# A two-layer graph kernel: where the block turns of the first hidden state stand in layer 1's first step

## The chip, the cores and the metric

The kernel runs on one core of one Trainium2 chip. The metric is the device time of one execution in microseconds. Five engines work side by side, each on its own queue: TensorE (PE, matmuls, with the weight loads listed apart as PEld), VectorE (DVE), ScalarE (ACT), GpSimd (POOL) and SyncE (SP), which here issues nearly all DMA transfers.

## What is computed

Sixteen batches of a 1024 x 128 matrix `x` go through two layers, all in float32. `adj` is a symmetric-pattern 1024 x 1024 matrix. Layer 0 is one graph convolution with a residual and a layer norm. Layer 1 is a gated graph unit that runs five steps, again with a residual and a layer norm:

```python
x = _layernorm(x + (adj @ (x @ w0) + b0))

def step(h, _):
    m_in = m_out = adj @ h            # in_matrix = out_matrix = adj
    av = jnp.concatenate([m_in, m_out], axis=-1)
    u3 = h @ u3_w.T + u3_b
    z = jax.nn.sigmoid(av @ w3_w.T + w3_b + u3)
    r = jax.nn.sigmoid(av @ w4_w.T + w4_b + u3)
    hv = jnp.tanh(av @ w5_w.T + w5_b + (r * h @ u5_w.T + u5_b))
    return (1.0 - z) * h + z * hv, None

h = x                                  # five steps
x = _layernorm(x + h)
```

The heavy part is the product `adj @ h`, once in layer 0 and five times in layer 1, for each of sixteen batches.

## The kernel before

**Tiling and stages.** The sixteen batches are worked on in four groups ("quads") of four. Layer 0 runs over the quads `q` = 0 to 3 first, and layer 1 then runs over the quads, five steps each. One step is an aggregation (`aggregate`, the product with `adj`) followed by the gates. The layer 0 projection of a quad is done inside the aggregation after it, through hooks: functions that are called at given places in the list of products. So layer 0's projection of the last quad falls into the aggregation of layer 1's first step (tag `0_0`), and it is in this stage that the change lies.

**The aggregation.** The product with `adj` is computed by a Strassen-Winograd scheme on two levels. The outer level has seven products, which run as four *chains*: (1, 2), (3,), (6, 7) and (5, 4). Each chain computes one or two outer products by seven inner products, in the order 1, 5, 6, 2, 7, 3, 4. The right-hand operands of the outer products 4 to 7 are sums that VectorE writes into `tsum`; the right-hand operands of the inner products 4 to 7 are four sums each, written by `inner_sums` (L328 to L331) into `inner0` for the chains (1, 2) and (6, 7), and into `inner1` for (3,) and (5, 4). Inner products are collected in three PSUM banks `pa`, `pc` and `pb`. When a product is finished it is evicted by a copy on ScalarE or by an addition on VectorE: L407 after product 1, L408 after 5, L409 after 6, L410 after 2 and L413 after 4 on ScalarE; L411 after 7 and L412 after 3 on VectorE. Product 3 reuses the bank of product 5, so it cannot start before L408 has emptied it.

**Where the results go.** The results of chain (6, 7) are written into `rows[:, 0:2]`, those of chain (5, 4) into `rows[:, 2:4]`. `rows` has until then held the quad's input, and in layer 1's first step this input is the first hidden state h, with nodes as rows. The gates need h in another layout, in `hid`. In every later step the gates themselves produce that layout; only the first h has to be brought there. This is what `to_hidden(k)` does for batch k of the quad: `turn_hidden` makes four block transposes ("turns", L643, each of 128 x 256) of `rows[:, k]` into two stage buffers in the upper halves of `agg`, sends each buffer to DRAM with one DMA (L647), and `fetch_hidden` reads it back into `hid[:, k]` with four DMAs (L655). The stage buffers are `agg[:, 2 * (k % 2) + f, HALF:]`, so batch 2 reuses those of batch 0 and batch 3 those of batch 1. Eight turns read `rows[:, 0]` and `rows[:, 1]`, eight read the other two. Until the turns of the rows 0 and 1 have run, chain (6, 7) may not write its first result there, which is L408.

**What sets the order.** A scheduler orders each engine's instructions; the place of a statement in the program is what it goes by first, and it may move an instruction forward where it expects a wait. Instructions that went through `keep_in_program_order` keep the program's order among themselves on their engine. In this stage the program has, in this order: the sums of chain (6, 7), chain (3,) with its hooks, the sums of chain (5, 4), chain (6, 7) with its hooks, chain (5, 4).

**The other work of the stage.** VectorE also does the statistics of layer 0's last layer norms (L267, L269). ScalarE applies them (L286, 128 x 128 each), in `ypad` for two batches and in place in `hid` for the other two, and SP stores those results to `saved` (L292) before `hid` is overwritten by the fetches of batches 2 and 3. The gates of the same step start right behind chain (5, 4) and read `hid` first in L535.

Of the kernel before, what the change touches and what calls it, by code (L numbers as in the profile page):

```python
# [20 lines left out]
def kernel(  # L21
# [32 lines left out]
    nc = tc.nc  # L54
# [3 lines left out]
    HALF = N // 2  # L58
# [13 lines left out]
    rows = const.tile([P, QUAD, N], F32, name="rows")  # L72
    hid = const.tile([P, QUAD, N], F32, name="hid")
    agg = const.tile([P, QUAD, N], F32, name="agg")
# [36 lines left out]
    def load(q, dst, src_of, ks=range(QUAD)):  # L111
        for k in ks:
            nc.sync.dma_start(dst[:, k], src_of(q * QUAD + k))
# [13 lines left out]
    for i, c in enumerate([0, 1, "x0", "x1", *range(2, C), "x2", "x3"]):  # L127
        queue = queues[i % 2 if i < 6 else 0]
        if isinstance(c, str):
            k = int(c[1])  # L130
# [222 lines left out]
    def outer_sums(src, early=True, late=True, pinned=False):  # L353

        lo, hi = src[:, 0:2], src[:, 2:4]
        put = tc.keep_in_program_order if pinned else lambda op: op
        if early in (True, "hi"):
            op = put(nc.vector.tensor_sub(tsum[:, 2], hi[:, :, HALF:], hi[:, :, :HALF]))
        if early in (True, "lo"):
            op = put(nc.vector.tensor_add(tsum[:, 1], tsum[:, 2], lo[:, :, :HALF]))  # L360
        if late:
            put(nc.vector.tensor_sub(tsum[:, 0], hi[:, :, :HALF], lo[:, :, :HALF]))
            op = put(nc.vector.tensor_sub(tsum[:, 3], lo[:, :, HALF:], tsum[:, 1]))
        return op

    def behind_closing():

        return tc.issue_after(closed[0].ins) if closed[0] else nullcontext()
# [173 lines left out]
    def gate_seed(u):  # L542
        pin(nc.scalar.copy(seeded[u % 2], pus[u]))
# [5 lines left out]
    def gate_r(u, rest=True):  # L549

        k, h = UNITS[u]
        rh, cols, pu = rh_of[k % 2], ts(h, HALF), pus.pop(u)
        in_order(nc.tensor.matmul(  # L553
            pu, w_t["w4"], agg[:, k, cols], start=False, stop=True, skip_group_check=True
        ))
        pin(nc.scalar.activation(rh[:, cols], pu, AF.Sigmoid, bias=br))  # L556
        if rest:
            gate_rh(u)

    def gate_rh(u):  # L560
        k, h = UNITS[u]
        rh, cols = rh_of[k % 2], ts(h, HALF)
        pin(nc.vector.tensor_mul(rh[:, cols], rh[:, cols], hid[:, k, cols]))  # L563

    def gate_z(u):
        k, h = UNITS[u]
        cols, pz = ts(h, HALF), seeded[u % 2]
        in_order(nc.tensor.matmul(  # L568
            pz, w_t["w3"], agg[:, k, cols], start=False, stop=True, skip_group_check=True
        ))  # L570
        pin(nc.scalar.activation(z_of[k % 2][:, cols], pz, AF.Sigmoid, bias=bz))  # L571
# [39 lines left out]
    def turn_rows(k, h=None, to=None):  # L611
        cols, n = half_of(h)
        to = between(k, h) if to is None else to
        t = ypad[k % 2][:, cols]
        op = nc.vector.transpose(
            t.rearrange("p (to n j c) -> p n to c j", to=4, n=n, c=2),
            hid[:, k, cols].rearrange("p (n to i c) -> p n to c i", to=4, n=n, c=2),
        )
        tc.keep_in_program_order(nc.sync.dma_start(
            to.rearrange("g p x -> p g x"), t.rearrange("p (g x) -> p g x", x=64)  # L620
        ))
        return op
# [8 lines left out]
                dst[ts(to, SQ), cols].rearrange("j (m x) -> j m x", x=64), src[to]  # L631
            ))

    def turn_hidden(k, y, stage):

        v = y.rearrange("p (n c a j) -> p a n c j", n=4, c=2, a=4)
        w = 4 // len(stage)
        for f, t in enumerate(stage):
            if w == 4:
                nc.vector.transpose(t.rearrange("p (a n i c) -> p a n c i", a=4, n=4, c=2), v)  # L640
            else:
                for a in range(w):
                    nc.vector.transpose(  # L643
                        t[:, ts(a, QT)].rearrange("p (n i c) -> p n c i", n=4, c=2),
                        v[:, w * f + a],
                    )
            nc.sync.dma_start(  # L647
                hidden[k][ts(f, 4 * w)].rearrange("g p x -> p g x"),
                t.rearrange("p (g x) -> p g x", x=64),
            )  # L650

    def fetch_hidden(k):
        src = hidden[k].rearrange("(a n) (b j) x -> a j (n b) x", a=4, b=4)
        for a in range(4):
            nc.sync.dma_start(  # L655
                hid[ts(a, SQ), k].rearrange("j (m x) -> j m x", x=64), src[a]
            )

    def to_hidden(k):
        turn_hidden(k, rows[:, k], [agg[:, 2 * (k % 2) + f, HALF:] for f in range(2)])  # L660
        fetch_hidden(k)

    def turn(name, k, h):
# [27 lines left out]
    def call(f, *args):  # L691
        return lambda: f(*args)


    def projections(q):

        room = rooms[q % 2]
        ys = [ypad[0], ypad[1], room[:, 2], room[:, 3]]
        for k in (2, 3):
            nc.sync.dma_start(ys[k], x_rows(q * QUAD + k))  # L700
        hooks = {a: [call(project, q, k, ys[k])] for k, a in enumerate((5, 2, 3, "end"))}
        hooks.update({a: [seed_bias] for a in (1, 6, 7, 4)})
        return hooks
# [246 lines left out]
    for q in range(NQ):  # L950
        for s in range(STEPS):
            tag = f"{q}_{s}"
            if s == 0:
                if q == 0:
                    hooks = {
                        12: projections(NQ - 1),
                        3: {5: [call(to_hidden, 0)], 2: [call(to_hidden, 1)]},
                        67: {
                            3: [call(drain, 99, 0), call(to_hidden, 2)],
                            "end": [call(to_hidden, 3)],  # L960
                        },
                        54: {},
                    }
                    hooks[12][6] += [call(sums_of, rows, (3,)), call(outer_sums, rows, False, True)]
                else:
                    outer_sums(rows)
                    hooks = {54: {}}
            else:
                hooks = {54: {}}
            last = s == STEPS - 1  # L970
            end = last and q == NQ - 1

            k = s if q else s - 1
            if q < NQ - 1 and 0 <= k < QUAD:
                hooks[3] = {1: [call(next_load, q + 1, k)]}
                hooks[67] = {1: [call(next_turn, k)]}
            if q > 0 and s > 0:
                hooks.setdefault(67, {})[5] = [call(close_load, q - 1, s - 1)]
                hooks[54] = {6: [call(close, q - 1, s - 1)]}
            if q == s == 0:  # L980
                hooks[54][3, (0,)] = [call(gates_begin, tag, 3)]
            hooks[54][4] = [call(gate_r, 0, False)]
            hooks[54][3, (1,)] = [call(gate_z, 0)]
            aggregate(tag, rows, hooks, s > 0)
            if end:
                load(q, rows, saved_rows)
            elif last:
                load(q + 1, rows, saved_rows)
            with behind_closing():
                gate_rh(0)  # L990
            if not end:
                gate_seed(2)
            gate_r(1)
            gate_z(1)
            if end:
                turns[0] = part_of[2]
                ending(q, tag)
                break

            def updated(k):  # L1000
                if last:
                    turn_rows(k, None, closing[k])
                    fetch_hidden(k)
                elif k < 3:
                    turn_rows(k)
                    if k < 2:
                        fetch_rows(k)

            def step_update(u, part):
                k, h = UNITS[u]  # L1010
                if last and u == 4:
                    sums_of(rows, (1, 2))
                    sums_of(rows, (3,))
                update_half(tag, k, h, part, not last and k == 3)
                if u % 2:
                    updated(k)

            for u in range(3, 8):
                gate_first(tag, u, (u - 3) % 3)
                step_update(u - 3, (u - 2) % 3)  # L1020
                gate_r(u - 1)
                gate_z(u - 1)
            step_update(5, 2)
            gate_r(7)
            gate_z(7)
            step_update(6, 0)
            step_update(7, 1)
            part_of.insert(0, part_of.pop())
            then = f"{q}_{s + 1}" if not last else f"{q + 1}_0"
            gates_begin(then, 2 if q == NQ - 1 and s == STEPS - 2 else 3)  # L1030
            if not last:
                fetch_rows(3, 1)
                fetch_rows(3, 0)
# [32 lines left out]
```

## Time and profile before

| | us |
|---|---|
| median of three runs | 1766.96 |
| lowest and highest run | 1766.76, 1766.97 |
| the profiled execution, whole | 1767.13 |
| its span, first to last instruction | 1764.9 |
| TensorE busy in the span | 1753.4 |
| VectorE busy | 1302.2 |
| ScalarE busy | 800.8 |

The span is what the trace shows; the whole time is a little longer. Times in the traces are microseconds from the span's start. The chains (6, 7) and (5, 4) of layer 1's first step lie at about 234 to 263 us.

A timeline line reads: start, duration, engine, source line, operation, output<-input, shape, count, and in brackets the idle time before it with what ended it. A line of the waits reads: who waited, for whom, then total us, times, longest. In the chain of waits a line is start, duration and what ran; "issue" stands for time in which nothing that the profile shows was waited for.

### The profile page before, as it was taken

How to read it: one execution, taken by the hardware profiler on the slowest of the kernel's cores; microseconds unless marked ns; L12 is line 12 of the kernel's file. 1: busy time of each engine (PE TensorE's matmuls, PEld its weight loads, DVE VectorE, ACT ScalarE, POOL GpSimd, SP SyncE). 2: the span in 40 equal slices, each digit the busy share in tenths (PEclk: the TensorE clock that was granted, in tenths of full speed). 3: DMA queues.
4: the chain of work that ended last, by engine and by line, in shares of the span. 5: the costliest groups of instructions: out<-in, count | busy, mean ns of one | idle time of the engine just before them, and what ended most of it. 6: DMA issues, size and time to landing. Idle time of an engine off the chain costs nothing.

```text
span 1764.9 us, 19957 instructions
## 1 busy us (share of the span) xinstructions
PE 1753.4 (99%) x6709; PEld 1264.9 (72%) x6709; DVE 1302.2 (74%) x2286; ACT 800.8 (45%) x1425; POOL 110.4 (6%) x153
## 2 busy tenths in 40 slices
PE   9999999999999999999999999999999999999998
PEld 8888885776858577685867758576675857668584
DVE  7977777676776857777778667777778577777778
ACT  4355554344353433435354452535445353443537
POOL 2312320000000000000000000000000000000004
PEclk9999999999999999999999999999999999999999
DMA  9244354051332505143351424324243240514232
GB/s 266 75 139 144 120 142 109 12 119 34 86 69 67 140 18 136 39 118 75 81 132 60 108 60 96 87 69 119 58 110 101 55 94 26 131 25 107 60 84 95
DMA packets 405604, 161.86 MB, mean 92 GB/s; under 512 B 388352, under 2 KB 389504, under 8 KB 405504
## 3 DMA queue, kind: packets, MB, share of 16 engines
q1 hardware_dynamic: 402960, 153.01, 34.2%
q0 software_dynamic: 1968, 5.77, 1.3%
q10 hardware_dynamic: 576, 1.84, 0.3%
q8 instruction: 53, 0.87, 0.2%
q14 instruction: 47, 0.39, 0.1%
HBM read 94.51 MB, written 65.01 MB: 90 GB/s over the span
## 4 chain that ended last, share of the span: by engine, by line
PE 99%; DMA 1%; DVE 0%; POOL 0%; issue 0%; SPq 0%; POOLq 0%; ACT 0%; DVEq 0%
PE pb L425 25%; PE pc L425 14%; PE pa L425 14%; PE pu L553 8%; PE ph L576 8%; PE ph L577 8%; PE pu L535 8%; PE seeded L568 8%; PE pc_x L425 3%; PE pa_x L425 3%; PE seeded L509 2%; DMA agg<-in_adj_dram 1%; PE pt_adj L200 0%; PE pt L667 0%; PE pt_end L941 0%
## 5 line engine op out<-in xcount | busy, mean ns | idle before, releaser
L425 PE MATMUL pb<-e,inner 128*128 128x256 f32 x864 | 206.2, 379 | 0.0
L592 DVE TENSOR_TENSOR tsum<-tsum,hid 128x512 f32<-128x512 f32 x158 | 108.7, 688 | 106.1 <-ACT tsum L587 106.0
L587 ACT ACTIVATE tsum<-ph,bh 128x512 f32<-128x512 f32 x158 | 108.5, 687 | 164.6 <-PE ph L577 164.5
L425 PEld LDWEIGHTS pb<-e,inner 128*128 128x128 f32 x864 | 167.7, 194 | 19.0 <-ACT first L409 0.3
L553 PE MATMUL pu<-agg,w_t 128*128 128x512 f32 x320 | 163.7, 593 | 0.0
L576 PE MATMUL ph<-agg,w_t 128*128 128x512 f32 x320 | 163.4, 592 | 0.0
L568 PE MATMUL seeded<-agg,w_t 128*128 128x512 f32 x320 | 163.4, 592 | 0.0
L577 PE MATMUL ph<-tsum,u_t 128*128 128x512 f32 x320 | 163.4, 592 | 0.0
L535 PE MATMUL pu<-hid,u_t 128*128 128x512 f32 x320 | 157.0, 592 | 0.0
L556 ACT ACTIVATE tsum<-pu,br 128x512 f32<-128x512 f32 x160 | 110.0, 687 | 85.6 <-PE pu L553 85.6
L425 PE MATMUL pb<-s,inner 128*128 128x256 f32 x576 | 148.0, 379 | 0.0
L425 PE MATMUL pb<-a,inner 128*128 128x256 f32 x576 | 144.0, 379 | 0.0
L563 DVE TENSOR_TENSOR tsum<-tsum,hid 128x512 f32<-128x512 f32 x160 | 110.3, 689 | 38.1 <-ACT tsum L556 38.1
L425 PE MATMUL pc<-e,inner 128*128 128x256 f32 x560 | 133.9, 379 | 0.0
L425 PEld LDWEIGHTS pb<-s,inner 128*128 128x128 f32 x576 | 110.7, 194 | 23.7 <-issue 10.9
L571 ACT ACTIVATE tsum<-seeded,bz 128x512 f32<-128x512 f32 x160 | 110.0, 687 | 29.4 <-PE seeded L568 29.4
L425 PEld LDWEIGHTS pb<-a,inner 128*128 128x128 f32 x576 | 111.8, 194 | 12.7 <-DVE first L411 0.4
L425 PEld LDWEIGHTS pc<-e,inner 128*128 128x128 f32 x560 | 109.2, 195 | 12.8 <-PE pu L535 0.7
L577 PEld LDWEIGHTS ph<-tsum,u_t 128*128 128x128 f32 x320 | 60.8, 190 | 76.5 <-issue 59.1
L576 PEld LDWEIGHTS ph<-agg,w_t 128*128 128x128 f32 x320 | 60.6, 190 | 75.1 <-issue 74.4
L535 PEld LDWEIGHTS pu<-hid,u_t 128*128 128x128 f32 x320 | 60.8, 190 | 73.5 <-issue 72.2
L593 DVE TENSOR_TENSOR tsum<-tsum 128x512 f32<-128x512 f32 x158 | 109.2, 691 | 4.9
(201 smaller groups left out, 2860.9 us busy)
## 6 DMA issues: line engine op xcount, KB each, us to landing
turned<-ypad SPq DMA_DIRECT2D x48, 512.0 KB, 3.8
rows<-turned SPq DMA_DIRECT2D x192, 128.0 KB, 2.9
hvs<-saved SPq DMA_DIRECT2D x24, 512.0 KB, 4.1
rows<-saved SPq DMA_DIRECT2D x20, 512.0 KB, 3.8
hid<-hidden SPq DMA_DIRECT2D x64, 128.0 KB, 3.4
turned<-ypad SPq DMA_DIRECT2D x32, 256.0 KB, 2.9
rows<-turned SPq DMA_DIRECT2D x128, 64.0 KB, 2.1
hidden<-ypad SPq DMA_DIRECT2D x12, 512.0 KB, 4.0
```

The costliest lines, as they stand in the source:

```text
L425: product = nc.tensor.matmul(bank_of[a][:, ts(o, QT)], chunk(a, o, c), left[n][a][:, c, :], start=(a in (1, 5) and o == 0 and c == 0), sto ...
L535: in_order(nc.tensor.matmul(pu, w_t["u3"], hid[:, k, ts(h, HALF)], start=True, stop=True, skip_group_check=True))
L553: in_order(nc.tensor.matmul(pu, w_t["w4"], agg[:, k, cols], start=False, stop=True, skip_group_check=True))
L556: pin(nc.scalar.activation(rh[:, cols], pu, AF.Sigmoid, bias=br))
L563: pin(nc.vector.tensor_mul(rh[:, cols], rh[:, cols], hid[:, k, cols]))
L568: in_order(nc.tensor.matmul(pz, w_t["w3"], agg[:, k, cols], start=False, stop=True, skip_group_check=True))
L571: pin(nc.scalar.activation(z_of[k % 2][:, cols], pz, AF.Sigmoid, bias=bz))
L576: in_order(nc.tensor.matmul(ph, w_t["w5"], agg[:, k, cols], start=True, stop=False))
L577: in_order(nc.tensor.matmul(ph, w_t["u5"], rh_of[k % 2][:, cols], start=False, stop=True))
L587: pin(nc.scalar.activation(hv, ph, AF.Tanh, bias=bh))
L592: pinned(nc.vector.tensor_sub(hv, hv, hid[:, k, cols]))
L593: pinned(nc.vector.tensor_mul(hv, hv, z_of[k % 2][:, cols]))
```

## The change

Three things are moved, and nothing is added to or taken from the work:

- The turns of batch 0, called by a hook of chain (3,) before its product 5, are called before product 1 of chain (6, 7). Those of batch 1, called before product 2 of chain (3,), are called before product 5 of chain (6, 7). Both then stand behind the sums of chain (5, 4) in the program.
- The turns of batch 2 keep their hook, before product 3 of chain (6, 7) and so behind the eviction of product 7, but now go through `keep_in_program_order`, so that they hold this place against other instructions that do the same.
- Batch 3 is unchanged.

```diff
-    def turn_hidden(k, y, stage):
+    def turn_hidden(k, y, stage, pinned=False):
...
                 for a in range(w):
-                    nc.vector.transpose(
+                    op = nc.vector.transpose(
                         t[:, ts(a, QT)].rearrange("p (n i c) -> p n c i", n=4, c=2),
                         v[:, w * f + a],
                     )
+                    if pinned:
+                        tc.keep_in_program_order(op)
...
-    def to_hidden(k):
-        turn_hidden(k, rows[:, k], [agg[:, 2 * (k % 2) + f, HALF:] for f in range(2)])
+    def to_hidden(k, pinned=False):
+        stage = [agg[:, 2 * (k % 2) + f, HALF:] for f in range(2)]
+        turn_hidden(k, rows[:, k], stage, pinned)
         fetch_hidden(k)
...
                         12: projections(NQ - 1),
-                        3: {5: [call(to_hidden, 0)], 2: [call(to_hidden, 1)]},
                         67: {
-                            3: [call(drain, 99, 0), call(to_hidden, 2)],
+                            1: [call(to_hidden, 0)],
+                            5: [call(to_hidden, 1)],
+                            3: [call(drain, 99, 0), call(to_hidden, 2, True)],
                             "end": [call(to_hidden, 3)],
                         },
```

In the built program this gives three differences. On VectorE the eight turns of batches 0 and 1, which stood together ahead of the sums of chain (5, 4), now stand behind L328, L330 and L329 of that chain: one of them, then L331, then the other seven. The turns of batch 2, which were spread around L331 and L411, now follow L411. On TensorE the first two matmuls of product 1 of chain (5, 4), which stood ahead of product 4 of chain (6, 7), now stand behind it. On ScalarE L413 of chain (6, 7) moves ahead by one L286. The order of the transfers on SP and of POOL's instructions is the same.

## The prediction

> **What bounds the kernel now.** I read the page first, then the chain of waits around the stage that the diff touches, then the timelines of VectorE, ScalarE and TensorE there. The page:
>
> ```profile
> PE 1753.4 (99%) x6709; PEld 1264.9 (72%) x6709; DVE 1302.2 (74%) x2286; ACT 800.8 (45%) x1425; POOL 110.4 (6%) x153
> ...
> PE 99%; DMA 1%; DVE 0%; POOL 0%; issue 0%; SPq 0%; POOLq 0%; ACT 0%; DVEq 0%
> ```
>
> TensorE is busy for 99% of the span and the chain that ended last is TensorE nearly throughout. So a microsecond in which TensorE stands still is a microsecond of the result, and work on another engine costs nothing until TensorE waits for it. The list of all waits has only four lines for TensorE in the whole run; three belong to the first 12 us. The fourth is the place of this change. The waits and the chain, both for 236 to 258 us:
>
> ```profile
> ACT rows L408 <- issue: 3.4, 1, 3.4
> ...
> PE pc L425 <- ACT rows L408: 0.3, 1, 0.3
> ```
>
> ```profile
> 239.13 1.37 issue
> 240.50 0.59 ACT rows L408
> 241.10 0.04 issue
> 241.14 1.13 PE pc L425 x4
> ```
>
> The reader is to see that ScalarE's L408 (it empties bank c after product 5 of chain 67) sat idle for 3.4 us for a reason which the profile does not name ("issue"), and that TensorE's product 3, which reuses bank c, then waited for L408. The timeline of VectorE shows what L408 was held by:
>
> ```profile
> 237.09 0.69 DVE L331 TENSOR_TENSOR inner<-tsum,inner 128x512 f32<-128x512 f32 x1
> 237.71 2.72 DVE L643 STREAM_TRANSPOSE agg<-rows 128x256 f32<-128x256 f32 x8
> 240.35 0.65 DVE L328 TENSOR_TENSOR inner<-tsum 128x512 f32<-128x512 f32 x1
> 240.92 0.68 DVE L330 TENSOR_TENSOR inner<-tsum 128x512 f32<-128x512 f32 x1
> 241.52 0.68 DVE L329 TENSOR_TENSOR inner<-tsum,inner 128x512 f32<-128x512 f32 x1
> 242.12 0.43 DVE L643 STREAM_TRANSPOSE agg<-rows 128x256 f32<-128x256 f32 x1
> 242.49 0.65 DVE L331 TENSOR_TENSOR inner<-tsum,inner 128x512 f32<-128x512 f32 x1
> 243.06 0.76 DVE L643 STREAM_TRANSPOSE agg<-rows 128x256 f32<-128x256 f32 x2
> 244.11 0.69 DVE L411 TENSOR_TENSOR rows<-pb,rows 128x512 f32<-128x512 f32 x1 [0.29 <-PE pb L425]
> ```
>
> The eight turns of batches 0 and 1 read `rows[:, 0]` and `rows[:, 1]`; L408 writes into those same two rows. The eighth turn ends at 237.71 + 2.72 = 240.43, L408 starts at 240.50. In the listing of the program's order L408 waits for a count of VectorE that the eighth turn supplies. TensorE's side:
>
> ```profile
> 238.95 1.03 PE L425 MATMUL pa<-s,tsum 128*128 128x256 f32 x4
> 239.82 1.03 PE L425 MATMUL pa<-a,tsum 128*128 128x256 f32 x4
> 241.14 1.13 PE L425 MATMUL pc<-e,tsum 128*128 128x256 f32 x4 [0.30 <-ACT rows L408]
> ```
>
> Four matmul records take 239.82 - 238.95 = 0.87 us from start to start, so product 3 could have begun at 240.69; it began at 241.14. The whole loss in this stage today is 0.45 us. That is also all that any reordering here can win on this wait.
>
> [...]L408's stall stopped ScalarE altogether from 237.1 to 240.5 us, with the evictions L409 and L410 behind it. [...]The trace before shows clock 1.00 even in the window 8 to 12 us, where TensorE was busy for only 2.79 of 4 us; a longer gap isn't shown. [...]here the issues of `hidden<-agg` land after a median of 3.7 us, and I use that.
>
> **The change part by part.** No instruction is added or removed; work only moves.
>
> *VectorE.* In the changed program's order the three sums L328, L330, L329 of chain 54 stand ahead of the first turn, then one turn, then L331, then the other seven turns of batches 0 and 1. L331 waits for the last product of chain 3, which ran near 233 us, so this wait is empty. From 237.71 the new sequence, with start-to-start times from the rows above: L328 0.57 (240.35 to 240.92), L330 0.60, L329 0.60, which puts the first turn at 239.48; turn 0.37 (242.12 to 242.49), L331 0.57 (242.49 to 243.06), so that the seven others begin at 240.42. A turn's pitch is (240.35 - 237.71)/8 = 0.33; seven take 2.31, and the last one ends 0.08 beyond its pitch, as now. The eighth turn ends at 240.42 + 2.31 + 0.08 = 242.81 in place of 240.43: 2.38 later.
>
> *ScalarE and TensorE.* L408 still waits for the eighth turn of rows 0 and 1: in the changed program its VectorE count is again supplied by just that turn. So L408 starts at 240.50 + 2.38 = 242.88 and product 3 at 241.14 + 2.38 = 243.52. TensorE has nothing else to do: its order before product 3 is the same in both programs[...]. The gap grows from 0.45 to 2.83 us. **This term, +2.38 us, is the forecast's core.** The sums that move forward win nothing: their first reader, product 5 of chain 54, runs at 248.15, over 5 us behind them.
>
> *Product 4 of chain 67.* In the changed order the two matmuls of the next chain's product 1 no longer stand between products 3 and 4. Product 4 needs bank b emptied by L411. Now product 7 issues until 243.84, L411 starts 0.27 later and takes 0.69, ending at 244.80; product 3's second half covers only up to 244.70, and the two matmuls covered the rest. Without them TensorE waits 244.80 + 0.05 - 244.70, about 0.15. Bounds: 0 to 0.3 us.
>
> *The cover behind it.* ScalarE runs back to back from 240.50 to 253.41 (three evictions, 24 L286 of about 0.40 each with L413 and L407 among them, then L408 and L409), and TensorE's product 7 of chain 54 already waits for that L409: records of 0.87 from 252.47 would reach it at 253.34, it begins at 253.46. The 0.15 above therefore goes partly into a wait that exists anyhow. Added up on ScalarE: four of the five L286 ahead of L413 are left, ready at 249.04; product 4 ends at 243.52 + 4 x 0.865 + 0.15 + 1.73 = 248.86, L413 at 249.12 (+0.08); three L286 and L407 end near 251.38; nine L286 and L408 bring L409 to 255.32, 0.11 over a pure shift of 252.83 + 2.38. So TensorE leaves the stage 2.38 + 0.1 = about 2.5 us late. Between 2.3 (no extra wait) and 2.8 (both extra waits in full).
>
> *The third batch's turn, pinned.* Its first turn waits for the landing of a store of batch 0 and now stands behind P7's eviction L411 rather than ahead of it. Before, it did not hold anything: L411 waited 0.29 us for TensorE and VectorE was otherwise busy. Gain 0. It now stands ahead of L412: the store, issued 2.38 later than at 238.49, lands near 240.87 + 3.7 = 244.6, while L411 starts at about 246.4. Cost 0; bounds 0 to 0.3.
>
> *SP's queue.* Its order is unchanged. The first store of a turned block is issued when its two turns are done, 240.83 in place of 238.45, so all eight stores and sixteen fetches slip by the same 2.4. Batch 1 of `hid` lands now near 248.5 + 3.1 = 251.6 and is first read at about 257.0; TensorE slips as far, so the margin of 5 us stays. The stores of batches 2 and 3 follow SP's `saved<-hid` copies, which follow ScalarE's L286, also 2.4 to 2.5 later. L489, at 262.13, needs the first of these landed (252.86 + 3.7 = 256.6): 5 us spare, both moving. POOL's queue isn't passed: its last L283 of the stage is done at 239.3.
>
> *The sum.* 1767.13 us (the profiled execution's own time; its span is 1764.9 and 2.2 lie around it) + 2.5 = 1769.6. The median of the runs, 1766.96, is 0.17 below the profiled run, so the median forecast is **1769.4**. That is 0.14% slower, really slower by the spread of 0.21 us of the runs, but within 0.2% (3.5 us), about what a measurement of this kernel can tell from no change.
>
> **The rivals.**
>
> *The clock falls in the new gap* (slower by more than 0.2%). Place: TensorE's gap of 2.83 us before product 3. [...]against it, [...]the 8 to 12 us stretch kept its clock. Chance 0.09.
>
> *A transfer is late.* If the slipped stores collide with the copies of `saved` and the hidden batch comes over 5 us late, gates wait: 1.5 to 3 us more, 1771 to 1772.5. For it: DMA is 0.89 busy from 240.6 to 255. Against: all users slip too. Chance 0.03.
>
> *L408 was held by something that does not move* (not slower). The profile calls the 3.4 us "issue" and names no releaser. Then the eviction stays at 240.50, product 3 at 241.14, and only the 0.15 of product 4 remains, mostly hidden: 1767.1; should the forward sums also free 0.45, 1766.5. Against it: the 0.07 us between the eighth turn's end and L408's start, and the program's count. Chance 0.06; none of this reaches 0.2% faster, for which I keep 0.01 of it.
>
> **How the numbers follow.** The forecast, 1769.4, has 0.82, by itself 1769.0 to 1769.9 (2.1 to 2.9 over the median, the bounds above and 0.2 for the runs' spread). With half of the clock rival's smaller cases [...]the range is 1768.7 to 1770.4. Slower by over 0.2% (above 1770.5) is 0.09 + 0.03 = 0.12; faster (below 1763.4) 0.01; the rest, 0.87, is the same.
>
> **What would show it.** VectorE: L328, L330, L329 from about 237.7, eight turns done near 242.8. L408 starting within 0.1 of that, with its idle of 3.4 grown to 5.8. A TensorE wait for L408 near 2.7 in place of 0.3; a small one for L411 ahead of product 4; then every later start shifted by a constant 2.4 to 2.6. It would be wrong if L408 starts before the eighth turn ends, if the clock column dips behind 243 us, or if TensorE gets new waits after 256 us.

## The result, and the profile after

| | before | changed |
|---|---|---|
| median of sixteen runs, us | 1766.96 | 1770.94 |
| lowest and highest | 1766.54, 1767.37 | 1769.34, 1772.12 |
| the profiled execution, whole | 1767.13 | 1769.38 |
| its span | 1764.9 | 1767.3 |

The changed kernel is slower: ratio 1.0022, 95% interval [1.0016, 1.0029]. That is 3.98 us, and the median lies above the forecast range (1768.7 to 1770.4). The spread matters as much as the median: the runs of the kernel before lie within 0.8 us, those of the changed one fall on two levels. Three lie at 1769.34 to 1769.38 us, thirteen at 1770.74 to 1772.12. The profile that came with the result is of a run on the *lower* level, and it shows what the forecast's sum said; the granted clock is 1.00 in every window from 236 to 260 us. Two of its waits from 236 to 262 us, and L408 in its chain of waits:

```profile
ACT rows L408 <- issue: 5.8, 1, 5.8
...
PE pc L425 <- ACT rows L408: 2.7, 1, 2.7
```

```profile
242.66 0.59 ACT rows L408
```

L408's idle time grew from 3.4 to 5.8 us, and TensorE's wait for it from 0.3 to 2.7. VectorE's timeline shows why:

```profile
237.46 0.68 DVE L328 TENSOR_TENSOR inner<-tsum 128x512 f32<-128x512 f32 x1
238.06 0.68 DVE L330 TENSOR_TENSOR inner<-tsum 128x512 f32<-128x512 f32 x1
238.66 0.68 DVE L329 TENSOR_TENSOR inner<-tsum,inner 128x512 f32<-128x512 f32 x1
239.27 0.43 DVE L643 STREAM_TRANSPOSE agg<-rows 128x256 f32<-128x256 f32 x1
239.63 0.64 DVE L331 TENSOR_TENSOR inner<-tsum,inner 128x512 f32<-128x512 f32 x1
240.20 2.39 DVE L643 STREAM_TRANSPOSE agg<-rows 128x256 f32<-128x256 f32 x7
246.25 0.69 DVE L411 TENSOR_TENSOR rows<-pb,rows 128x512 f32<-128x512 f32 x1 [3.67 <-PE pb L425]
```

The eighth turn ends at 240.20 + 2.39 = 242.59 and L408 starts at 242.66, again 0.07 us behind. VectorE then has nothing to do for 3.67 us: all that was pulled forward was taken from a place where it cost nothing. TensorE in the same profile:

```profile
239.56 1.03 PE L425 MATMUL pa<-a,tsum 128*128 128x256 f32 x4
243.30 1.13 PE L425 MATMUL pc<-e,tsum 128*128 128x256 f32 x4 [2.71 <-ACT rows L408]
...
246.00 1.03 PE L425 MATMUL pc<-e,tsum 128*128 128x256 f32 x4
247.00 1.13 PE L425 MATMUL pb<-s,inner 128*128 128x256 f32 x4
```

Product 3 could have begun at 239.56 + 0.87 = 240.43 and began at 243.30, a gap of 2.87 us (0.45 before). Product 4 began at 247.00 and not at 246.87: 0.13 us for L411. From 256 to 300 us TensorE waited for nothing. So this profile explains the lower level, 2.4 us over the median before, and nothing of the 1.4 to 2.8 us more that most runs took.

### The profile page after: what moved, and what is told of

The parts are those of the page before. It is cut to its first block, busy times and chain, and to the rows that moved or that the text cites. A ratio compares the mean times of both kernels' runs of the same rounds, so it can differ in the third digit from the quotient of the medians.

```text
span 1767.3 us, 19957 instructions
## 1 busy us (share of the span) xinstructions
PE 1754.5 (99%) x6709; PEld 1266.7 (72%) x6709; DVE 1302.4 (74%) x2286; ACT 801.4 (45%) x1425; POOL 111.5 (6%) x153
## 4 chain that ended last, share of the span: by engine, by line
PE 99%; DVE 0%; issue 0%; POOL 0%; POOLq 0%; ACT 0%; DVEq 0%
PE pb L425 25%; PE pc L425 14%; PE pa L425 14%; PE pu L553 8%; PE ph L576 8%; PE pu L535 8%; PE ph L577 8%; PE seeded L568 8%; PE pc_x L425 3%; PE pa_x L425 3%; PE seeded L509 2%; PE pt_adj L200 0%; PE seeded L212 0%; PE pt L670 0%; PE pb L212 0%
## 5 line engine op out<-in xcount | busy, mean ns | idle before, releaser
L280 POOL TENSOR_SCALAR rstd<-mv 128x8 f32<-128x8 f32 (+1 forms) x32 | 12.5, 390 | 1613.8 <-DVE mv L269 1578.7
```

## The experiments

Two theories stood for the upper level. C: the array's clock falls in or right behind the new gap. This is the forecast's first rival. L: something behind the gap, a transfer or a wait, comes late. Each kernel below was timed beside the kernel before, on the same chip.

**The changed kernel again**, to get a profile of the upper level.

> The changed kernel itself, once more. Its sixteen runs fell on two levels: three at 1769.3 to 1769.4 us, thirteen at 1770.7 to 1772.1. Theory C (the clock): the 2.7 us gap of TensorE before product 3 makes the array's clock fall in most executions; again two levels, about 1769.4 and 1771.1, and if the profile falls on the upper one its clock column is below 1 [...]behind 243 us, with no new wait anywhere and later starts shifted by another 1.4 to 2.0 us. Theory L (something later): the upper level comes from a transfer or wait behind the gap, as the hidden batches' fetches; then a profile of the upper level shows clock 1.00 there and a TensorE wait of 1.4 to 2 us behind 256 us.

Ten runs, median 1771.20 us against 1767.09 (ratio 1.0022 [1.0012, 1.0031]): three at 1769.47 to 1769.88, one at 1770.37, six at 1771.12 to 1772.66. The profiled execution took 1771.28 us, the upper level. Its windows of 2 us (length, then busy time and count for each engine, the granted clock, the DMA share and GB/s):

```profile
core 0: us, PE busy (x) PEld busy (x) DVE busy (x) ACT busy (x) POOL busy (x), PEclk, DMA share, GB/s
242.00:244.00 2.00, 0.16 (x1) 0.16 (x2) 1.12 (x4) 0.80 (x2) 0.00 (x0) 1.00 0.90 199
244.00:246.00 2.00, 2.00 (x8) 1.70 (x9) 0.00 (x0) 2.00 (x6) 0.00 (x0) 0.78 0.94 199
246.00:248.00 2.00, 2.00 (x6) 1.55 (x6) 0.00 (x0) 2.00 (x6) 0.00 (x0) 0.50 1.17 249
248.00:250.00 2.00, 2.00 (x10) 1.68 (x9) 1.76 (x4) 1.36 (x4) 0.00 (x0) 0.86 1.21 251
250.00:252.00 2.00, 2.00 (x11) 1.77 (x10) 2.00 (x6) 0.99 (x3) 0.00 (x0) 1.00 0.51 118
```

Read the clock's column (third from the right): 0.78, 0.50 and 0.86 behind the gap, then 1.00. The loss is 2 x (0.22 + 0.50 + 0.14) = 1.72 us, which is a clock of 0.50 for 3.44 us. TensorE is "busy" all through; only its count per window falls, from 11 to 6. The chain shows the same without the clock: product 7's eight records take 3.13 us in place of 1.73.

```profile
244.97 3.13 PE pb L425 x8
248.10 1.15 PE pc L425 x4
249.25 1.73 PE pb L425 x8
```

The wait for L408 in this execution is 2.7 us, as in the lower level's, and there is no TensorE wait between 256 and 300 us. C is shown for this execution, and L has no place in it.

**The gap filled.**

```diff
+    def fill():
+        for _ in range(5):
+            tc.keep_in_program_order(nc.tensor.matmul(
+                seeded[0][:, :QT], ident, agg[:, 0, :QT], start=True, stop=True,
+                skip_group_check=True,
+            ))
...
                         67: {
                             1: [call(to_hidden, 0)],
                             5: [call(to_hidden, 1)],
+                            2: [fill],
```

> The changed kernel with five matmuls of 128x256 whose result nobody reads, between products 6 and 2 of chain (6, 7), into a bank that is free there: 5 x 0.43 = 2.2 us of work that fits into the gap of 2.7 us. The turns, L408 and every transfer stay where they are. Theory C: the gap shrinks to about 0.5 us, the clock stays, all runs fall on one level at 1769.2 to 1769.6 us. Theory L: nothing behind the gap has changed, two levels as before, median 1770.9.

Twenty-one runs, all within 1769.30 to 1769.86, median 1769.59 against 1767.09 (ratio 1.0014 [1.0007, 1.0021]). TensorE did some 2.2 us *more* work than in the changed kernel (an estimate, 5 x 0.43: in the profile of the kernel with two such matmuls, below, the two took 0.86 us) and the upper level was gone. The eviction stayed where the turns put it (L408 at 242.93, 0.08 us behind the eighth turn), the stores and fetches behind it came as late as in the changed kernel, which speaks against L. Only TensorE's wait for L408 shrank:

```profile
PE pc L425 <- ACT rows L408: 0.6, 1, 0.6
```

**A shorter gap.** L467 of this stage is called by a hook before product 2 of chain (6, 7) in place of its old line, so it comes behind the turns.

```diff
             if not sums67:
-                nc.vector.tensor_add(agg[:, 0:2, :HALF], ...)
+            if not sums67 and tag != "0_0":
+                nc.vector.tensor_add(agg[:, 0:2, :HALF], ...)
...
+                            2: [first_half],
```

> The changed kernel with one more move: the addition L467 (128x1024, 1.13 us from start to start), which stood ahead of the turns on VectorE and whose result is first read by the gates, goes behind the eight turns. L408 comes 1.13 earlier, the gap falls from 2.7 to about 1.6 us. Theory C[...]: no slow level left, or very few runs, median 1768.2 us. Theory L: both levels move by 1.13, median 1769.8.

Thirteen runs within 1768.31 to 1768.85, median 1768.50 (ratio 1.0008 [0.9999, 1.0016]); the wait for L408 was 1.6 us. The gap's plain price stayed, the second level did not.

**A longer gap.** L467 is done twice in its old place.

```diff
-            if not sums67:
+            for _ in range(0 if sums67 else 2 if tag == "0_0" else 1):
                 nc.vector.tensor_add(agg[:, 0:2, :HALF], ...)
```

> The changed kernel with L467 of this stage done twice: 1.13 us more of VectorE work ahead of the turns, the gap grows to about 3.9 us. Plain shift: 1769.35 + 1.13 = 1770.5 for a run whose clock stays. Theory C: [...]1771.7 to 1772.6 and no run on the lower level. Theory L: two levels in the same shares as before, 1770.5 and 1772.1.

Six runs, 1771.93 to 1773.18, median 1772.43 (ratio 1.0030 [1.0018, 1.0042]), wait 3.8 us. None lies near 1770.5, the plain shift. In its profile the clock fell while TensorE was still idle:

```profile
242.00:244.00 2.00, 0.00 (x0) 0.00 (x0) 2.00 (x7) 0.00 (x0) 0.00 (x0) 0.77 0.42 92
244.00:246.00 2.00, 1.15 (x3) 0.97 (x4) 0.14 (x1) 1.79 (x4) 0.00 (x0) 0.50 0.97 217
246.00:248.00 2.00, 2.00 (x7) 1.55 (x5) 0.40 (x2) 2.00 (x7) 0.00 (x0) 0.50 1.04 222
248.00:250.00 2.00, 2.00 (x6) 1.64 (x5) 0.80 (x3) 2.00 (x7) 0.00 (x0) 0.53 1.22 240
```

The loss of the column is 2 x (0.23 + 0.50 + 0.50 + 0.47) = 3.40 us, a clock of 0.50 for 6.80 us: about twice the 3.44 us of the upper level above. If the fall is put at the end of the first of these windows, 0.92 us before 244.00, TensorE stood still for the first 1.77 us of it (product 3 began at 244.85), so the matmuls lost about (6.80 - 1.77)/2 = 2.5 us (an estimate from these two figures; this execution took 1772.79 us, 2.3 over the plain shift). The single runs at 1772.12, 1772.66 and, below, 1772.54 us, each the slowest of its set with a stop of 2.7 us, may be of this kind; none of them was profiled.

**Between: two matmuls and one in the gap** (the fill above with `range(2)` and `range(1)`).

> The changed kernel with two of the unread matmuls in place of five: 0.87 us of the gap is filled and about 1.85 us are left. Theory C [...]which left no slow run at 1.64 us and most at 2.75: two levels again, 1769.5 and 1771.2, with a third to two thirds of the runs on the upper one. If the limit lies higher (say over 2 us), one level at 1769.5[...].

> The changed kernel with a single unread matmul of 128x256 in the gap: about 2.25 us of it are left. A gap of 1.85 us left no run slow, one of 2.75 made most slow. Theory C [...]for 2.25 us a share of 0.66[...]. If the limit is sharper than this[...], the share here is well under a half. Levels 1769.5 and 1771.2. Theory L: most runs at 1771.

With two, 21 runs lie within 1769.21 to 1770.17, median 1769.71 (ratio 1.0015 [1.0008, 1.0021]), wait 1.8 us: no upper level, against the first expectation. With one, 17 runs split into nine at 1769.37 to 1769.80 and eight at 1771.01 to 1771.91, median 1769.80 (ratio 1.0019 [1.0012, 1.0026]), wait 2.3 us. So a wait of 1.8 us put none of 21 runs on the upper level and one of 2.3 us eight of 17. The profile of the kernel with one matmul is of the lower level and keeps the clock at 1.00.

**The gap without the change**: the kernel before, with L467 three times.

> The kernel before, its turns where they were, with L467 of this stage done three times: 2.26 us more VectorE work ahead of the turns and so a gap of about 2.7 us as in the changed kernel. Theory C: the clock loss belongs to the gap and not to the change: two levels, about 1769.3 and 1771.1, the upper one in most runs. Theory L (a transfer or wait that the move of the turns makes late): one level at 1769.3.

Twenty-one runs, six at 1768.86 to 1769.72 and fifteen at 1770.54 to 1771.50, median 1770.83 against 1766.98 (ratio 1.0020 [1.0013, 1.0027]); wait 2.6 us. The turns keep their place in the program, and the time is that of the changed kernel. The profile is of the upper level, and its clock column reads 0.93, 0.50 and 0.72 from 242 to 248 us. So the loss belongs to the gap and not to the new order. By itself this does not exclude L, because the turns and their stores run late here too; what excludes it are the fills with five and with two matmuls, where they run as late and no run is on the upper level.

**The pin by itself, and the change without it.** The first takes `True` out of the changed kernel's hook, the second puts the hooks of batches 0 and 1 back:

```diff
-                            3: [call(drain, 99, 0), call(to_hidden, 2, True)],
+                            3: [call(drain, 99, 0), call(to_hidden, 2)],
```

```diff
+                        3: {5: [call(to_hidden, 0)], 2: [call(to_hidden, 1)]},
                         67: {
-                            1: [call(to_hidden, 0)],
-                            5: [call(to_hidden, 1)],
```

> The changed kernel without the pin on the third batch's turns; its four turns then stand ahead of L411 on VectorE, two of them behind waits for the landing of stores. If the pin is worth nothing, as predicted, the time is that of the changed kernel: two levels at 1769.4 and 1771.2, the upper one in most runs, and L411 starts where it does now. If the pin saves something, L411 (246.25 in the changed kernel's profile) comes later by the wait for the store, up to 0.5 us, and both levels move up by as much.

> The kernel before with the pin on the third batch's turns alone; the turns of batches 0 and 1 stay in chain (3,). If all of the loss comes from their move, this is the kernel before within 0.2 us, on one level, with a gap of 0.45 us before product 3. If the pin or the order behind it has a share in the loss, it is slower by that share.

Without the pin: five runs at 1769.27 to 1769.67, eight at 1770.83 to 1772.54, median 1770.86 (ratio 1.0020 [1.0012, 1.0028]), the changed kernel's two levels. Its profile is of the upper level: the clock column reads 0.54 and 0.60 from 244 to 248 us, a clock of 0.50 for 3.44 us again. All four turns of the third batch stand ahead of L411 there, and two waits for stores stand in front of them:

```profile
243.47 0.77 DVE L643 STREAM_TRANSPOSE agg<-rows 128x256 f32<-128x256 f32 x2 [0.80 <-DMA hidden<-agg]
244.67 0.77 DVE L643 STREAM_TRANSPOSE agg<-rows 128x256 f32<-128x256 f32 x2 [0.42 <-DMA hidden<-agg]
248.02 0.69 DVE L411 TENSOR_TENSOR rows<-pb,rows 128x512 f32<-128x512 f32 x1 [2.58 <-ACT ypad L286]
```

They end at 245.44, before L411 could have begun even with the clock at 1.00 (246.25 in the changed kernel), so they hold nothing. (L411 itself is late there because product 7 took 3.21 us in place of 1.73; the bracket's releaser is an inference.) The pin alone: thirteen runs, 1766.97 to 1768.14, median 1767.19 against 1767.10 (ratio 1.0001 [0.9993, 1.0009]), wait 0.3 us. With the change or without it, no effect of the pin can be told from zero.

**The kernel before without its gap**: the kernel before with L467 behind the eight turns, the same edit as in "A shorter gap".

> The kernel before with L467 of this stage behind the eight turns. L408 comes about 1.1 us earlier, at 239.4 in place of 240.5, and its bank is free before product 2 ends. If the gap of 0.45 us in the kernel before is held by the turns alone, it is gone and the median falls by 0.4 to 0.5 us, to 1766.5 to 1766.6. If something else holds product 3 there, the time stays at 1767.0.

> The kernel before with L467 behind the eight turns, once more: its first comparison gave 1766.29 against 1767.10 us, a gain of 0.8 where the gap of 0.45 was expected. If the gain is real it comes again, 0.6 to 0.9 us, with no TensorE wait for L408. If the part over 0.45 was the chip's drift, the gain is 0.3 to 0.5.

> The same with the change's pin on the third batch's turns. If the pin is worth nothing here as well, 1766.2 to 1766.4 us, as without it; if its eviction of product 7 comes sooner for it, up to 0.2 us less.

First time 1766.29 against 1767.10 us (thirteen runs, 1765.94 to 1766.73), again 1766.36 against 1766.94 (1765.80 to 1766.74), with the pin 1766.30 (1765.96 to 1767.15). The ratios are 0.9996 [0.9987, 1.0004], 0.9996 [0.9988, 1.0004] and 0.9997 [0.9988, 1.0005], so the intervals do not exclude no change; that three sets of runs agree, and that the first one's runs lie at or below the lowest of the 49 beside them, speaks for a gain of 0.6 to 0.8 us. In the first one's trace L408 still starts right behind the eighth turn (236.76 + 2.40 = 239.16), so the bracket's "PE pb", an inference, is hardly what released it. But it comes 1.3 us earlier than in the kernel before, and TensorE waits for it no more:

```profile
236.76 2.40 DVE L643 STREAM_TRANSPOSE agg<-rows 128x256 f32<-128x256 f32 x7
239.24 0.59 ACT L408 COPY rows<-pc 128x512 f32<-128x512 f32 x1 [2.25 <-PE pb L425]
```

The scheduler also changed TensorE's order in all three: product 7 (240.55) now stands ahead of product 3 (242.28), so the gain is that of L467's new place and this order together. The gain is over the 0.45 us of the gap; the traces show a small loss at the end of a stop, too. The four records behind a stop took 0.97 us from start to start (241.14 to 242.11 and 253.46 to 254.43 in the kernel before) in place of 0.87. Two such stops are nearly all gone, the one before product 3 and one of 0.12 us before product 7 of chain (5, 4). With what they cost at their ends, 0.10 and 0.07, this is 0.45 + 0.12 + 0.17 = 0.74 us in the traces.

**The gap and the clock together:**

| kernel | wait for L408, us | runs | on the upper level |
|---|---|---|---|
| changed, five matmuls in the gap | 0.6 | 21 | 0 |
| changed, L467 behind the turns | 1.6 | 13 | 0 |
| changed, two matmuls | 1.8 | 21 | 0 |
| changed, one matmul | 2.3 | 17 | 8 |
| before, L467 three times | 2.6 | 21 | 15 |
| changed | 2.7 | 16 | 13 |
| changed, again | 2.7 | 10 | 6, and one between |
| changed, no pin | 2.7 | 13 | 8 |
| changed, L467 twice | 3.8 | 6 | 6 |

The wait is that of the one profiled execution, and the level of a run is read from its time. The four profiles of the upper level (changed again, no pin, L467 three times, L467 twice) show a clock down to 0.50 behind or in the gap; the five others in this table keep 1.00 there.

## Why the prediction was wrong

*The sum of the moved instructions was right in the main.* The forecast had the eighth turn end 2.38 us later; the profile has 242.59, which is 2.42 later once the 0.26 us are allowed for by which TensorE had come to this stage earlier (239.56 against 239.82). The gap was to grow from 0.45 to 2.83 and grew to 2.87. Product 4's wait for L411 was to be 0.15 and is 0.13. The pin was put at 0 and showed no effect. The hidden batches' transfers slipped and met no waiting TensorE. Lower level: 1769.4 forecast, 1769.34 to 1769.38 in the result's three runs, 1769.59 with the gap filled. That it was hit so closely is partly luck. By the profile the stage cost 257.70 - 255.29 + 0.26 = 2.67 us at its end, where the forecast had 2.5: L411's wait was not hidden, and the stop before product 4 cost another 0.10 at its end, a term that the forecast did not have.

*What failed is the step that set the clock rival aside*, with a chance of 0.09. The rival's sign came: the clock column dips behind 243 us, and the profile of the upper level lost 1.72 us by it. That a gap of 2.83 us would leave the clock alone was the author's estimate, which no trace of the kernel before showed. The one observation given for it, "the 8 to 12 us stretch kept its clock", was no evidence for a longer gap, since the 1.21 us of idle time in that stretch lie in two gaps, of 0.61 and 0.60 us, both below the 1.8 us that left all of 21 runs on the lower level:

```profile
8.61 1.96 PE L425 MATMUL pa_x<-a,rows 128*128 128x256 f32 x8 [0.61 <-DMA rows<-in_x_dram]
11.17 2.18 PE L200 MATMUL pt_adj<-ident,agg 128*128 128x128 f32 x16 [0.60 <-DMA agg<-in_adj_dram]
```

A wait of 2.3 us put 8 of 17 runs on the upper level and one of 2.7 us 27 of 39.

*Why two levels.* What decides in one execution whether the clock falls was not shown. The runs show the share on the upper level by the wait: none of 21 at 1.8 us, 8 of 17 at 2.3, 15 of 21 at 2.6, 27 of 39 at 2.7 and 6 of 6 at 3.8. The profiles show how long the fall lasted: by their clock columns 3.44, 3.44 and 3.40 us at a clock of 0.50 in the three with waits of 2.7, 2.7 and 2.6 us, and 6.80 us in the one with a wait of 3.8. The single run at 1770.37 us stays unexplained.

*The third rival*, that L408 was held by something that does not move, is out: in all the kernels here it started 0.07 to 0.09 us behind the end of the eighth turn, from 239.24 us with L467 behind the turns to 244.21 with L467 twice.

## What to carry to other kernels

A turn that only reads a buffer still holds whoever writes this buffer next (here L408, 0.07 us behind the eighth turn); before moving such work behind other work, look for the first eviction into what it reads, and move the work that no one waits for (here L467) behind it instead. Price a new stop of TensorE twice: its length, and what the clock may lose behind it: here 1.70 to 1.72 us in three profiles of the upper level, on which none of 21 runs lay at a wait of 1.8 us, 8 of 17 at 2.3 and 27 of 39 at 2.7. Where runs of one kernel fall on two levels, read the clock's column window by window, since a mean over the whole execution (0.997 or 0.998 on the upper level, 0.998 or 0.999 before) hides it, and one profile may be of the wrong level.

## What was not expected of the hardware

With a wait of 2.3 us 8 of 17 runs were on the upper level, with one of 2.7 us 27 of 39; the profiles of that level with waits of 2.6 and 2.7 us show a clock of 0.50 for 3.40 to 3.44 us, some 1.7 us lost. In the one profile with a wait of 3.8 us it lasted 6.80 us. Five matmuls whose result nobody reads made the changed kernel 1.6 us faster in the median (1769.59 against 1771.20, timed side by side). And in the traces of both kernels TensorE took 0.1 us longer over the first four records behind a stop (0.97 against 0.87 us from start to start), with the clock column at 1.00.
